# A four-layer graph attention stack: ScalarE issues the 2048-piece reads, GpSimd takes the roots, and the planner counts transfers differently

## The chip, the cores and the metric

The kernel runs on one core of a Trainium2 chip. The metric is the device time of one launch in microseconds (us). Engines are named as in the profile: PE is TensorE (PEld its weight loads), DVE VectorE, ACT ScalarE, POOL GpSimd, SP SyncE, which here only issues DMAs. Each engine executes its own instructions in order and waits on semaphores for the others.

## The reference

128 independent graphs of 128 nodes with 512 features pass through four attention layers. Each layer is an attention over a masked 128x128 score matrix (with 1, 4, 8 and 1 heads), a residual and a layer norm:

```python
x = _layernorm(x + _L0_gnn_ref(x, adj, ...), axis=-1)   # 1 head, no projection, mask adj + I
x = _layernorm(x + _L1_gnn_ref(adj, x, ...), axis=-1)   # 4 heads of 256, elu, then 1 head of 512
x = _layernorm(x + _L2_gnn_ref(x, adj, ...), axis=-1)   # 8 heads of 64
x = _layernorm(x + _L3_gnn_ref(x, adj, ...), axis=-1)   # 1 head of 32 for the scores, elu
```

A layer norm is (x - mean) / sqrt(var + 1e-5) over the 512 features. An attention is, head by head,

```python
e = leaky_relu(s_i[:, None] + s_j[None, :], 0.2)
a = softmax(where(mask, e, -big))
y = a @ h
```

All data are fp32.

## The kernel before

One graph is one tile of 128 partitions (its nodes) by 512 columns. Everything that happens to one graph, from the load of x to the store of the result, is written once in `graph(g)` as a list of `Op`s with an engine, a cost in us, a function that emits the instructions, and the buffers read and written. Some weights are loaded and prepared in a `setup` list, which is interleaved with the first graphs.

The order in which each engine gets its instructions isn't the order of the text. `Pipeline` makes it in two steps, both in Python while the kernel is built:

- `plan` takes one graph and lays its operations on a cycle of `PERIOD` us, by a list schedule with a random shift for each operation (`SEED`, `SPREAD`) and a weight for what is still behind it (`URGENCY`). Graph g gets the same times plus g periods. `Op.done` adds the `LATENCY` of the engine before a reader may start.
- `order` takes the operations of all 128 graphs and the setup and issues them one after the other as an imagined machine would: each engine has a clock, `FLOW` is the latency from one engine to another, `lane` is the one resource that all transfers share (`dma` us each), and a buffer is given to an operation only when a slot is free. An operation may be taken up to `AHEAD` us ahead of the earliest one not yet issued. The sequence that comes out is the instruction stream; on the chip semaphores hold the dependencies, whatever the times turn out to be.

So the constants change no computation, but they change the order on all five engines at once. Some fifteen graphs are under way at any time.

What matters for the change, with line numbers of the profile:

- Attention. `spread` turns a score column into a row through DRAM: a VectorE transpose (L589), a DMA to `row` (L592), a DMA that broadcasts the row to all partitions (L596). `attend` adds the other score and applies the leaky relu on ScalarE (L646, one instruction a head), masks and takes the minimum on VectorE (L654), exponentiates on ScalarE (L663), takes reciprocals (L671) and, for layers 1 and 3, scales on GpSimd (L673).
- Transposes. `turned` transposes 128x128 blocks for TensorE: VectorE transposes 32x32 blocks (L607), SyncE writes them to a DRAM scratch tile `scr` (L612) and reads them back with the blocks in their new places (L622, or L617 where `moving`). With n = 4 the read at L622 is made of 128 x 16 pieces of 32 elements, 2048 in all; there are four of these a graph: the transposed x before the projections at L710 with w1s and with wha, and the two halves of the 8 heads for L938. With n = 1 it has 512 pieces.
- Layer norm. `norm` has statistics on VectorE (L681, L682), the root as exp(-0.5 ln(var + eps)) on ScalarE (L685, L686), -mean times root on GpSimd (L692), and the scaling of the 128x512 tile on ScalarE (L699). There are four a graph.
- Matmuls. L710 projections, L725 mixing with 512 columns, L794 the second matrix of layer 1 (seven products for two graphs in place of eight), L850 the transpose of a mask, L896 and L938 mixing of heads. ScalarE evicts the projections (L717).
- The masks are made on GpSimd from adj (L838, L738), and GpSimd does several 128x512 additions (L780, L862, L881, L950, L986).

Before, SyncE issues every transfer of a graph, 30 in all. A transfer signals one of eight DMA semaphores, taken in turn, so an issue also waits until the transfer eight before it has landed.

Of the kernel before, what the change touches and what calls it, by code (L numbers as in the profile page):

```python
# [29 lines left out]

PERIOD = 28.0
LATENCY = {"PE": (0.0, 0.8), "DVE": (0.15, 1.44), "ACT": (0.1, 1.44), "POOL": (0.1, 1.44), "SP": (7.06, 7.06)}
FLOW = {"PE": (0.0, 0.6), "DVE": (0.15, 0.8), "ACT": (0.1, 0.8), "POOL": (0.1, 0.8), "SP": (4.5, 4.5)}
AHEAD = 20.0
URGENCY = 0.6
BANKS = 8

SEED, SPREAD = 989, 8.0

# [21 lines left out]
class Op:  # L61
# [8 lines left out]
    def done(self, reader=None):  # L70
        own, other = LATENCY[self.engine]
        return self.cost + self.extra + (own if reader is self.engine else other)


class Pipeline:
# [69 lines left out]
    def order(self, events):  # L145

        ops, n = [e[3] for e in events], len(events)
# [33 lines left out]
        known = {e: [i for i in range(n) if not before[i] and ops[i].engine == e] for e in FLOW}  # L181
        issued, low, out = [False] * n, 0, []

        def start(i):
            t = max(clock[ops[i].engine], ready[i])
            for b in makes[i]:

                rank = 0
                for q in coming[b.tag]:
                    if q >= i or rank >= len(free[b.tag]):  # L190
                        break
                    rank += 1
                if rank >= len(free[b.tag]):
                    return None
                t = max(t, free[b.tag][rank][0])
            return t

        while len(out) < n:
            best = None
            for e, waiting in known.items():  # L200
                found = None
                for i in waiting:
                    if events[i][0] > events[low][0] + AHEAD and i != low:
                        break
                    t = start(i)
# [6 lines left out]
            t, i = best  # L212
            op = ops[i]
# [7 lines left out]
            own, other = FLOW[op.engine]  # L221
            if op.engine == "POOL":
                other += op.extra
            if op.dma:

                done = lane = max(lane, done) + op.dma
                own = other = FLOW["SP"][0]
            for q in after[i]:
                ready[q] = max(ready[q], done + (own if ops[q].engine == op.engine else other))
                before[q] -= 1  # L230
                if not before[q]:
                    insort(known[ops[q].engine], q)
# [11 lines left out]
def tile_gat_stack(  # L244
# [50 lines left out]
    nc.scalar.preload_act_table_set("natural_log_exp_and_others")  # L295
    minus = const.tile([P, P], F32, name="minus")
# [270 lines left out]
    def graph(g):  # L567
# [3 lines left out]
        def op(engine, cost, emit, ins=(), outs=(), extra=0.0, uses=(), dma=0.0):  # L571
            ops.append(Op(engine, cost, emit, list(ins), list(outs), extra, uses, dma))
# [7 lines left out]
        def spread(col, nh):  # L580


            sT, row = Buf(f"sT{nh}", [P, nh, 32]), Buf(f"row{nh}", [nh, P])

            def turn():
                c, out = col(), sT.ap
                if len(c.shape) > 2:
                    out = out.rearrange("p (a b) c -> p a b c", a=c.shape[1])
                nc.vector.transpose(out, c.unsqueeze(len(c.shape)).to_broadcast([*c.shape, 32]))  # L589

            op("DVE", 0.12 + 0.033 * nh, turn, [col.buf], [sT])
            op("SP", 0.6, lambda: nc.sync.dma_start(  # L592
                out=row.ap.rearrange("h (b c) -> b h c", b=P // 32), in_=sT.ap[0:P:32]
            ), [sT], [row], dma=0.02 + 0.03 * nh)
            db = Buf(f"db{nh}", [P, nh, P])
            op("SP", 0.4, lambda: nc.sync.dma_start(  # L596
                out=db.ap.rearrange("p h j -> p (h j)"),
                in_=row.ap.rearrange("h j -> (h j)").partition_broadcast(P),
            ), [row], [db], 1.0 + 0.1 * nh, dma=0.03 + 0.19 * nh)
            return db  # L600

        def turned(src, n, moving=False):
# [8 lines left out]
            ), [src], [zb])  # L611
            op("SP", 0.4, lambda: nc.sync.dma_start(  # L612
                out=scr.ap, in_=zb.ap.rearrange("p b h c -> p (b h c)")
            ), [zb], [scr], 0.2 * n, dma=0.05 + 0.17 * n)
# [7 lines left out]
            op("SP", 0.65, lambda: nc.sync.dma_start(  # L622
                out=out.ap.rearrange("p h (q c) -> p h q c", q=4),
# [13 lines left out]
        def attend(db, h0, nh, src, mask, scaled=False):  # L637
# [192 lines left out]
        def first(g):  # L830


            x0, at = Buf("x0", [P, F]), Buf("adj", [P, P], I32)
            op("SP", 0.4, lambda: nc.sync.dma_start(out=x0.ap, in_=x[g]), [], [x0], 1.0, dma=0.72)
            op("SP", 0.4, lambda: nc.sync.dma_start(out=at.ap, in_=adj[g]), [], [at], 1.0, dma=0.22)
            ae = Buf("ae", [P, P], I32)
# [18 lines left out]

            resid(x1, pa, ri, x0)
            norm(x1)


# [4 lines left out]
        def second(g, st, xl):  # L864
# [46 lines left out]
        def third(g, st, xl2):  # L911
# [48 lines left out]

            op("DVE", 0.2, scores, [z3, xl3], [sc4])
            mv, rd = norm(x3, plus=1.0)
# [11 lines left out]
            at, m3 = Buf("adj", [P, P], I32), Buf("m3", [P, P])  # L974
            op("SP", 0.4, lambda: nc.sync.dma_start(out=at.ap, in_=adj[g]), [z3], [at], 1.0, dma=0.22)
            mask(m3, at, ALU.is_equal)
# [10 lines left out]
            norm(y)  # L987
            op("SP", 0.4, lambda: nc.sync.dma_start(out=out[g], in_=y.ap), [y], [], 1.0, dma=0.72)
        if g == B:
# [61 lines left out]
```

## Time and profile before

| | |
|---|---|
| median of 3 runs | 3223.14 us (3217.84 to 3232.31) |
| profiled execution | 3260.22 us, span 3258.4 us |
| mean granted TensorE clock | 0.976 |
| DMA: moved, mean busy share of the queue over 16 engines | 606.08 MB, 75.0% |
| SyncE: transfers issued in its program order | 3873 |
| VectorE waits in all, the longest kind: L744 for x from DRAM | 85.0 us in 71 times |

| us from the start | PE | DVE | ACT | POOL |
|---|---|---|---|---|
| 0 to 100 | 73.47 | 52.14 | 30.91 | 53.83 |
| 100 to 200 | 86.58 | 72.72 | 47.67 | 64.23 |
| 1000 to 1100 | 96.46 | 89.02 | 79.77 | 58.12 |
| 2000 to 2100 | 96.39 | 88.81 | 76.36 | 60.93 |
| 3100 to 3200 | 77.63 | 76.98 | 75.68 | 34.36 |

The second table is busy time in us in stretches of 100 us. The kernel fills for some 200 us, runs evenly to 3100 us, and drains. Every duration below comes from the profiled execution, which took 1.0115 times the median of the runs. Numbers in a group's line are the busy time as a union, the mean of one instruction in ns, and the idle time of the engine just before such instructions. Matmul records come in two for each fp32 matmul.

### The profile page before, as it was taken

The page shows a single profiled execution, that of the slowest core. Times are in us where ns is not written, and L with a number is a line of the kernel's source. Part 1 is how long each engine was busy: PE and PEld are TensorE (multiplying, and loading weights), DVE is VectorE, ACT ScalarE, POOL GpSimd, SP SyncE. Part 2 cuts the span into 40 slices and gives each one's busy share as a digit, 9 for nine tenths or more (in the row PEclk, how much of TensorE's full clock was granted, in tenths as well). Part 3 has the DMA queues.
Part 4 walks back from the last instruction along what each step waited for, and adds up shares of the span by engine and source line. Part 5 has one row for each costly group of instructions (what it writes and reads, how often), then busy time and mean ns, then how long its engine had stood idle before and what let it go on. Part 6 is the DMA issues. An engine that isn't in the chain of part 4 may idle for free. (4 is left out here: it accounts for less than half of the span.)

```text
span 3258.4 us, 62058 instructions
## 1 busy us (share of the span) xinstructions
PE 3066.8 (94%) x14822; PEld 2488.7 (76%) x14822; DVE 2779.0 (85%) x9833; ACT 2451.2 (75%) x8741; POOL 1895.1 (58%) x2347
## 2 busy tenths in 40 slices
PE   6899999999999999999999999999999999999984
PEld 4688887787777877877777778777787777878853
DVE  4779888888888988898888889889898898989875
ACT  2457787787777777787777877777877777778875
POOL 4655655665565655665555665565566556565533
PEclk7899999999999999999999999999999999999985
DMA  4358777877877877877778777877787787777875
GB/s 119 94 136 196 183 205 188 200 193 190 203 187 188 205 186 192 201 190 200 188 187 200 191 188 204 189 190 201 191 204 187 188 205 188 196 196 190 197 174 129
DMA packets 1657567, 606.08 MB, mean 186 GB/s; under 512 B 1311562, under 2 KB 1508170, under 8 KB 1657204
## 3 DMA queue, kind: packets, MB, share of 16 engines
q1 hardware_dynamic: 1655836, 598.97, 75.0%
q8 instruction: 120, 1.97, 0.2%
q14 instruction: 243, 1.99, 0.2%
q0 software_dynamic: 576, 2.10, 0.2%
q10 hardware_dynamic: 792, 1.06, 0.1%
HBM read 374.43 MB, written 227.48 MB: 185 GB/s over the span
## 5 line engine op out<-in xcount | busy, mean ns | idle before, releaser
L710 PE MATMUL ps<-w1s,w 128*128 128x258 f32 x4096 | 926.9, 384 | 48.5 <-DMA w<-scr 25.0
L710 PEld LDWEIGHTS ps<-w1s,w 128*128 128x128 f32 x4096 | 777.0, 191 | 186.3 <-DVE xl L812 39.5
L654 DVE CUSTOM_DVE_ANT_0 w<-w,w 128x128 f32<-128x128 f32 x1920 | 861.1, 544 | 65.6 <-ACT w L646 49.2
L794 PE MATMUL ps<-w2s,w 128*128 128x257 f32 x3584 | 849.0, 383 | 8.5 <-POOL w L780 8.4
L663 ACT ACTIVATE w<-w,nm 128x128 f32<-128x128 f32 x1920 | 748.0, 394 | 98.2 <-DVE nm L654 76.3
L794 PEld LDWEIGHTS ps<-w2s,w 128*128 128x128 f32 x3584 | 669.1, 191 | 188.8 <-issue 80.0
L646 ACT ACTIVATE w<-w,xl 128x128 f32<-128x128 f32 x1536 | 488.8, 389 | 279.9 <-DMA w<-row 259.1
L607 DVE STREAM_TRANSPOSE w<-w 128x512 f32<-128x512 f32 (+1 forms) x1024 | 551.5, 540 | 34.3 <-ACT w L663 13.3
L710 PE MATMUL ps<-wha,w 128*128 128x273 f32 x2048 | 502.3, 398 | 7.3 <-DMA w<-scr 6.9
L710 PEld LDWEIGHTS ps<-wha,w 128*128 128x128 f32 x2048 | 383.2, 192 | 87.4 <-DVE w L607 6.3
L699 ACT ACTIVATE w<-w,mr,rd 128x512 f32<-128x512 f32 x512 | 415.2, 811 | 33.9 <-POOL mr L692 33.0
L692 POOL TENSOR_SCALAR mr<-mv,rd 128x1 f32<-128x1 f32 x512 | 160.1, 313 | 409.4 <-ACT rd L686 201.8
L663 ACT ACTIVATION_READ_ACCUMULATOR w<-w,nm 128x1 f32 x1920 | 368.1, 192 | 0.0
L681 DVE BATCH_NORM_STATS2 st<-w 128x6 f32<-128x512 f32 x512 | 337.2, 668 | 5.4 <-POOL w L986 4.6
L881 POOL TENSOR_TENSOR xl<-xl,b1t 128x512 f32<-128x512 f32 x256 | 335.2, 1310 | 1.6
L938 PEld LDWEIGHTS ps<-xl,w 128*128 128x128 f32 x2048 | 274.3, 196 | 80.8 <-issue 24.4
L646 ACT ACTIVATE w<-w,sc 128x128 f32<-128x128 f32 x384 | 152.3, 397 | 227.6 <-DMA w<-row 226.6
L725 PE MATMUL ps<-w,w 128*128 128x512 f32 x512 | 277.4, 624 | 32.6 <-DMA w<-scr 31.6
L738 POOL TENSOR_SCALAR w<-adj 128x128 f32<-128x128 int32 x256 | 192.4, 752 | 188.2 <-DMA adj<-in_adj_dram 75.1
L717 ACT COPY xl<-ps 128x258 f32<-128x258 f32 (+1 forms) x768 | 273.2, 362 | 31.8 <-PE ps L710 31.3
L938 PE MATMUL ps<-xl,w 128*128 128x66 f32 x2048 | 265.2, 273 | 27.7 <-DMA w<-scr 14.4
L654 DVE DVE_READ_ACCUMULATOR2_ANT nm<- 128x1 f32 x1920 | 290.5, 151 | 0.0
(213 smaller groups left out, 4258.8 us busy)
## 6 DMA issues: line engine op xcount, KB each, us to landing
scr<-w SPq DMA_DIRECT2D x640, 256.0 KB
w<-scr SPq DMA_DIRECT2D x640, 256.0 KB
w<-row SPq DMA_DIRECT2D x128, 512.0 KB
w<-in_x_dram SPq DMA_DIRECT2D x128, 256.0 KB
w<-row SPq DMA_DIRECT2D x128, 256.0 KB
out_dram<-w SPq DMA_DIRECT2D x128, 256.0 KB
w<-row SPq DMA_DIRECT2D x384, 64.0 KB
scr<-w SPq DMA_DIRECT2D x384, 64.0 KB
```

Of the source, the lines that this page charges most:

```text
L607: op("DVE", 0.12 + 0.133 * n, lambda: nc.vector.transpose(zb.ap.rearrange("p b h c -> p h b c"), src.ap.rearrange("p (h b c) -> p h b c", ...
L646: nc.scalar.activation(z.ap[:, h, :], db.ap[:, h0 + h, :], AF.Prelu, bias=src(h0 + h), alpha=SLOPE)
L654: nc.vector.tensor_tensor_reduce(out=zz.ap[:, h, :].rearrange("p (b a) -> p a b", b=4), in0=z.ap[:, h, :].rearrange("p (a b) -> p a b", b= ...
L663: nc.scalar.activation(zz.ap[:, h, :], zz.ap[:, h, :], AF.Exp, bias=nm.ap[:, h : h + 1], scale=-1.0, accum_out=rs.ap[:, h : h + 1],)
L681: op("DVE", 0.6, lambda: nc.vector.bn_stats(st.ap, y.ap), [y], [st])
L699: op("ACT", 0.7, lambda: nc.scalar.activation(y.ap, y.ap, AF.Identity, bias=mr.ap, scale=rd.ap), [y, rd, mr], [y])
L710: op("PE", w * 4 / 2400 + 0.006, lambda k=k: nc.tensor.matmul(px.ap[:, :w], lhsT=lhs.ap[:, k, :], rhs=wa(k, c), start=(k == 0), stop=(k == ...
L717: op("ACT", 0.06 + w / 1200, lambda: nc.scalar.copy(dst(), px.ap[:, :w]), [px], [t])
L725: op("PE", width * 4 / 2400, lambda: nc.tensor.matmul(pa.ap[:, :width] if len(xv.shape) == 2 else pa.ap.rearrange("p (s c) -> p s c", s=2) ...
L794: return lambda: nc.tensor.matmul(q[b].ap[:, :C2], lhsT=x()[:, k, :], rhs=w2s[:, slot, k, :], start=(fresh and k == 0), stop=(k == 3), ski ...
L881: op("POOL", 1.3, lambda nh=nh: nc.gpsimd.tensor_add(xl.ap[:, nh, : 2 * FH], xl.ap[:, nh, : 2 * FH], b1t[:, nh * 2 * FH : (nh + 1) * 2 * F ...
L938: op("PE", 0.225, lambda u=u, h=h: nc.tensor.matmul(pa.ap[:, u * CH : (u + 1) * CH], lhsT=pt.ap[:, u, :], rhs=xl3.ap[:, h * CH : (h + 1) * ...
```

## The change

The reads of `turned` with n = 4 are issued from ScalarE's DMA queue. The root of the layer norm is one addition and one power on GpSimd, and the table preload on ScalarE goes. The first norm of a graph is scaled by one VectorE instruction in place of GpSimd's and ScalarE's. Of the two evictions of the wha projection one goes to VectorE. The planner gets other constants: a period, latencies, urgency and seed; longer costs for issuing transfers; a window of eight transfers (`WINDOW`, `LANDING`) outside which no issue may start; the latency of a transfer for any operation with `dma`, whoever issues it; and new costs for a few operations on GpSimd and VectorE.

```diff
-PERIOD = 28.0
-LATENCY = {"PE": (0.0, 0.8), "DVE": (0.15, 1.44), "ACT": (0.1, 1.44), "POOL": (0.1, 1.44), "SP": (7.06, 7.06)}
-FLOW = {"PE": (0.0, 0.6), "DVE": (0.15, 0.8), "ACT": (0.1, 0.8), "POOL": (0.1, 0.8), "SP": (4.5, 4.5)}
+PERIOD = 30.0
+LATENCY = {"PE": (0.0, 0.8), "DVE": (0.15, 1.76), "ACT": (0.1, 1.76), "POOL": (0.1, 1.76), "SP": (6.98, 6.98)}
+FLOW = {"PE": (0.0, 0.6), "DVE": (0.15, 0.8), "ACT": (0.1, 0.8), "POOL": (0.1, 0.8), "SP": (3.2, 3.2)}
 AHEAD = 20.0
-URGENCY = 0.6
+WINDOW, LANDING = 8, 2.0
+URGENCY = 0.3
 BANKS = 8
-SEED, SPREAD = 989, 8.0
+SEED, SPREAD = 139, 8.0
...
-        own, other = LATENCY[self.engine]
+        own, other = LATENCY["SP" if self.dma else self.engine]
...
             t = max(clock[ops[i].engine], ready[i])
+            if ops[i].dma and ops[i].engine != "POOL" and len(landed) >= WINDOW:
+                t = max(t, landed[-WINDOW])
...
-            if op.engine == "POOL":
-                other += op.extra
             if op.dma:
 
                 done = lane = max(lane, done) + op.dma
                 own = other = FLOW["SP"][0]
+                if op.engine != "POOL":
+                    landed.append(done + LANDING)
+            elif op.engine == "POOL":
+                other += op.extra
...
-    eps = const.tile([P, 1], F32, name="eps")
-    nc.vector.memset(eps, EPS)
-    nc.scalar.preload_act_table_set("natural_log_exp_and_others")
+    neghalf = const.tile([P, 1], F32, name="neghalf")
+    nc.vector.memset(neghalf, -0.5)
...
-            op("SP", 0.6, lambda: nc.sync.dma_start(
+            op("SP", 0.64, lambda: nc.sync.dma_start(
...
-            op("SP", 0.4, lambda: nc.sync.dma_start(
+            op("SP", 0.52, lambda: nc.sync.dma_start(
...
-                op("SP", 0.6, lambda: nc.sync.dma_start(
+                op("SP", 0.52, lambda: nc.sync.dma_start(
...
-            op("SP", 0.65, lambda: nc.sync.dma_start(
+            by, cost, queue = ("ACT", 0.7, nc.scalar) if n == 4 else ("SP", 0.75, nc.sync)
+            op(by, cost, lambda: queue.dma_start(
                 out=out.ap.rearrange("p h (q c) -> p h q c", q=4),
                 in_=flat().rearrange("(q p h c) -> p h q c", q=4, p=P, h=n),
             ), [scr], [out], 1.5, dma=0.415 * n)
...
-                op("POOL", 0.15 + 0.29 * nh, lambda: nc.gpsimd.tensor_mul(
+                op("POOL", 0.15 + 0.22 * nh, lambda: nc.gpsimd.tensor_mul(
...
-        def norm(y, plus=0.0):
+        def norm(y, plus=0.0, on_act=True):
...
             def root():
-                nc.scalar.activation(rd.ap, mv.ap[:, 1:2], AF.Ln, bias=eps)
-                nc.scalar.activation(rd.ap, rd.ap, AF.Exp, scale=-0.5)
-
-            op("ACT", 0.44, root, [mv], [rd])
+                nc.gpsimd.tensor_scalar_add(rd.ap, mv.ap[:, 1:2], EPS)
+                nc.gpsimd.tensor_tensor(out=rd.ap, in0=rd.ap, in1=neghalf, op=ALU.pow)
+
+            op("POOL", 0.95, root, [mv], [rd])
+            if not on_act:
+                op("DVE", 0.45, lambda: nc.vector.tensor_scalar(
+                    out=y.ap, in0=y.ap, scalar1=mv.ap[:, 0:1], scalar2=rd.ap,
+                    op0=ALU.subtract, op1=ALU.mult,
+                ), [y, mv, rd], [y])
+                return
...
-            norm(x1)
+            norm(x1, on_act=False)
...
-                op("POOL", 1.3, lambda nh=nh: nc.gpsimd.tensor_add(
+                op("POOL", 1.36, lambda nh=nh: nc.gpsimd.tensor_add(
...
-            project(xT, lambda k, c: wha[:, k, c * C3 // 2 : (c + 1) * C3 // 2], KF, C3 // 2, xl3, ["ACT", "ACT"],
+            project(xT, lambda k, c: wha[:, k, c * C3 // 2 : (c + 1) * C3 // 2], KF, C3 // 2, xl3, ["DVE", "ACT"],
...
-            op("DVE", 0.2, scores, [z3, xl3], [sc4])
+            op("DVE", 0.7, scores, [z3, xl3], [sc4])
```

The other transfers on SyncE (x, adj, the writes to `scr`, the store) go from a cost of 0.4 to 0.52 in the same way. In the new program order SyncE issues 3361 transfers and ScalarE 512 of those 2048-piece reads.

More of the change, by code (lines that the diff above doesn't have):

```diff
@@ L181, in order @@
         known = {e: [i for i in range(n) if not before[i] and ops[i].engine == e] for e in FLOW}
-        issued, low, out = [False] * n, 0, []
+        issued, low, out, landed = [False] * n, 0, [], []
         def start(i):
             t = max(clock[ops[i].engine], ready[i])
+            if ops[i].dma and ops[i].engine != "POOL" and len(landed) >= WINDOW:
+                t = max(t, landed[-WINDOW])
             for b in makes[i]:
@@ L611, in turned @@
             ), [src], [zb])
-            op("SP", 0.4, lambda: nc.sync.dma_start(
+            op("SP", 0.52, lambda: nc.sync.dma_start(
                 out=scr.ap, in_=zb.ap.rearrange("p b h c -> p (b h c)")
@@ L616, in turned @@
             if moving:
-                op("SP", 0.6, lambda: nc.sync.dma_start(
+                op("SP", 0.52, lambda: nc.sync.dma_start(
                     out=out.ap.rearrange("p h i -> p (h i)").rearrange("p (q e) -> p q e", q=4),
@@ L833, in first @@
             x0, at = Buf("x0", [P, F]), Buf("adj", [P, P], I32)
-            op("SP", 0.4, lambda: nc.sync.dma_start(out=x0.ap, in_=x[g]), [], [x0], 1.0, dma=0.72)
-            op("SP", 0.4, lambda: nc.sync.dma_start(out=at.ap, in_=adj[g]), [], [at], 1.0, dma=0.22)
+            op("SP", 0.52, lambda: nc.sync.dma_start(out=x0.ap, in_=x[g]), [], [x0], 1.0, dma=0.72)
+            op("SP", 0.52, lambda: nc.sync.dma_start(out=at.ap, in_=adj[g]), [], [at], 1.0, dma=0.22)
             ae = Buf("ae", [P, P], I32)
@@ L974, in third @@
             at, m3 = Buf("adj", [P, P], I32), Buf("m3", [P, P])
-            op("SP", 0.4, lambda: nc.sync.dma_start(out=at.ap, in_=adj[g]), [z3], [at], 1.0, dma=0.22)
+            op("SP", 0.52, lambda: nc.sync.dma_start(out=at.ap, in_=adj[g]), [z3], [at], 1.0, dma=0.22)
             mask(m3, at, ALU.is_equal)
@@ L987, in third @@
             norm(y)
-            op("SP", 0.4, lambda: nc.sync.dma_start(out=out[g], in_=y.ap), [y], [], 1.0, dma=0.72)
+            op("SP", 0.52, lambda: nc.sync.dma_start(out=out[g], in_=y.ap), [y], [], 1.0, dma=0.72)
         if g == B:
```

## The prediction

> **What bounds the kernel now.** I read the busy shares first, then a long steady stretch cut out of the span, then what TensorE waits for in it, then how the other engines lose time.
>
> ```profile
> PE 3066.8 (94%) x14822; PEld 2488.7 (76%) x14822; DVE 2779.0 (85%) x9833; ACT 2451.2 (75%) x8741; POOL 1895.1 (58%) x2347
> ```
>
> ```profile
> 300.00:3000.00 2700.00, 2609.49 (x12856) 2135.26 (x12855) 2376.62 (x8493) 2115.03 (x7597) 1613.76 (x2008) 1.00 0.79 194
> ```
>
> The columns of the second line are PE, PEld, DVE, ACT and POOL busy us, then clock, DMA share and GB/s. One graph has 115 matmul records (32+28+16+16+16+6+1 from the groups' counts divided by 128), so 12856 records are 111.8 graphs: 24.15 us a graph, in which PE is busy 23.34, DVE 21.26, ACT 18.92, POOL 14.43. PE idles 90.5 us of the 2700, 0.81 us a graph. TensorE bounds the kernel, and nothing can save more than 0.81 x 128 = 104 us outside fill and drain.
>
> ```profile
> PE ps L710 <- DMA w<-scr: 25.0, 24, 2.1
> PE ps L725 <- DMA w<-scr: 15.2, 27, 1.3
> PE ps L850 <- DVE w L903: 15.0, 15, 1.9
> PE ps L710 <- DVE ri L671: 9.3, 9, 2.1
> PE ps L710 <- DVE st L681: 8.4, 5, 2.0
> ```
>
> These are TensorE's waits from 300 to 3000 us (total, times, longest). 40.2 us hang on reads of transposed data, of which 25.0 on the 2048-piece ones (L710); most of the rest hangs on VectorE. At 85 to 88% busy, VectorE is next after TensorE, and part of its busy time is no work:
>
> ```profile
> L654 DVE CUSTOM_DVE_ANT_0 w<-w,w x1920: 328/382/1522, 33.4 to 3241.2; 128x128 f32<-128x128 f32 x192
> L959 DVE TENSOR_TENSOR sc<-sc,xl x128: 160/563/1201, 264.6 to 3231.0; 128x2 f32<-128x2 f32 x128
> ```
>
> ```profile
> 1002.07 1.27 POOL L780 TENSOR_TENSOR w<-w,w 128x512 f32<-128x512 f32 x1
> 1002.09 0.15 DVE L654 DVE_READ_ACCUMULATOR2_ANT nm<- 128x1 f32 x1
> 1002.09 1.50 DVE L654 CUSTOM_DVE_ANT_0 w<-w,w 128x128 f32<-128x128 f32 x1
> ```
>
> Min/median/max in ns: the same 128x128 masking takes 0.33 us or 1.5 us, and the long one began just as GpSimd's 1.27 us tensor_tensor did. Its mean is 544 ns in the groups, so 1920 x (544-382) = 311 us are excess; L959 adds 128 x (638-160) = 61 us, two elements wide as it is.
>
> Last, the issuing:
>
> ```profile
> 1005.02 0.64 SPq L622 DMA_DIRECT2D w<-scr  x1
> ```
>
> ```profile
> 0.73 1.28 ACT L295 ACT_TABLE_LOAD   x1 [0.73 <-PEq L1037]
> 0.77 0.53 ACTq L318 DMA_DIRECT2D w_-1_1_95<-in_L_gnn_attn_w_dst_dram  x1
> ```
>
> ```profile
> ACT w L646 <- DMA w<-row: 485.7, 319, 7.8
> ```
>
> A 2048-piece read holds SyncE 0.64 us, plus about 0.1 us between two issues (gaps of 0.03 to 0.05 us around a short semaphore instruction). ScalarE's sequencer can issue a DMA while its engine works (0.77 lies inside the table load). And ScalarE already waits 485.7 us, in order, for broadcast rows.
>
> **What the Trainium skill says.** "SBUF — State Buffer", section "SBUF: two separate sides": VectorE and GpSimd share a port pair under an exclusive lock; a VectorE instruction with two SBUF inputs, or in a two-port mode, and a GpSimd one shut each other out for the whole instruction. The trace agrees (0.33 against 1.50 us). "DMA: Bandwidth & Descriptors", section "Issuing engines are not separate DMA queues": a second issuing engine saves only the sequencer's issue time. The trace has nearly all transfers on one queue, so it can't say; I take it that data flows no faster. "VectorE: DVE Perf Modes", section "Mode 2×_2P": fp32 tensor_scalar from SBUF can do two elements a cycle; no steady instruction here shows it.
>
> **The change, part by part.** Sums stand against the profiled execution, 3260.22 us (span 3258.4), 1.0115 times the median of 3223.14; I divide by that at the end.
>
> *Reads to ScalarE.* 512 issues (4 a graph) leave SyncE: 512 x 0.74 = 379 us of its queue, 12% of the span. ScalarE gets them: between 0, where the issue lies under a running activation, and 379 us; I take 0.64 x 512 = 328, because each also waits for its write to land and for one of the eight semaphores, with evictions and exps queued behind it.
>
> *Roots to GpSimd.* ScalarE loses 146.4 + 103.8 = 250 us (L685, L686). GpSimd gets 512 adds at 0.27 us (L692's median for one column) and 512 powers. No power runs in the trace: at least 0.27 us like the add, at most 0.68, which would make the pair the 0.95 us booked for it in the code. I take 0.5: 512 x 0.77 = 394 us (276 to 486). One hop between engines goes (VectorE, GpSimd, ScalarE in place of VectorE, ScalarE, GpSimd, ScalarE); the chain's work is 0.49 us before and 0.77 after, so its length hardly moves.
>
> *First norm on VectorE, one L710 eviction of wha to VectorE.* ScalarE loses 128 x 0.811 + 128 x 0.369 = 151 us, GpSimd 128 x 0.313 = 40. VectorE gets 128 tensor_scalars of 128x512: 0.33 us at two a cycle (estimate, 512/0.96 GHz/2 + 60 ns, from the page's clock and rate) to 0.73 (L733, the nearest row); I take 0.45, so 58 us. And 128 copies of 273 columns at 0.40 (L812 moves 257 in 0.404): 51 us.
>
> *The lock.* GpSimd goes from 1895 to 1895+394-40 = 2249 us, 19% more. The excess of 311+61 = 372 us on VectorE grows between 0 (short instructions block briefly) and 19%, 71 us; I take 50.
>
> *Sums per engine.* ScalarE 2451-250-151+328 = 2378. GpSimd 2249 (69%). SyncE gains 379. VectorE 2779+58+51+50 = 2938, +1.24 us a graph: 22.50 of 24.15, 93%. TensorE's work is the same, matmul for matmul.
>
> *The order.* All queues are reordered, so single waits can't be followed across. What the two instruction orders tell: a tile's running number counts tiles placed so far, some 350 a graph, so the distance from a read's tile to its first matmul is a share of a graph. For the 512-wide mixing (L725) the nearest distances go from 0.21 to 0.45 of a graph, for the mask transpose (L850) from 0.27 to 0.35; for the w1 projection (L710, the largest wait) from 0.285 to 0.286. For ScalarE's four-head L646, which waits for broadcasts, the median falls from 0.265 to 0.18, or 6.4 to 4.4 us. So TensorE gets more room at two of its three waits, and ScalarE less. The lag from a graph's mask transpose to its last mixing stays (15.86 to 15.62 graphs of TensorE work), so fill and drain stay: nothing booked.
>
> *Queue for queue.* The most that earlier reads give is 40.2 x 128/111.8 = 46 us. Against it stands VectorE's room: 24.15-21.26 = 2.89 us idle a graph now, 1.24 of it taken. If VectorE's waits shrink by all 1.24, nothing is lost; if by none, 1.24 x 128 = 159 us. Much of its idle time is being early, for x (85.0 us at L744) or a free row tile (51.7 at L589), and that shrinks; waits inside chains with ScalarE and TensorE don't. I choose that five sixths are absorbed: 0.20 us a graph lost, 26 us, with the reads' gain used up by VectorE coming later to evictions and residuals. So 3260+26 = 3286, over 1.0115: **3249 us**.
>
> **Rivals.** *A, the reads win:* VectorE's idle time takes all 1.24 us and TensorE loses its read waits: 3260-46 = 3214, 3177 us by the median (3150 to 3207). For it: TensorE's stalls are short (2.1 us at most) and the order gives them room; chains behind them are mostly transfers. Against: it needs TensorE at 98% and VectorE at 94 to 95% in one in-order machine with eight PSUM banks. *B, a wash:* a read can't start before its write has landed, whoever issues it, and the wait moves along: 3223. For it: SyncE's L622 waited for its write only 26.7 us in all, so SyncE was seldom the cause. *C, ScalarE becomes late:* L646 sits behind 2 us less distance and a blocking read. If half of its 768 waits for broadcasts cost 0.5 us more and TensorE pays half of that, +96 us: 3318. It decides once ScalarE's 24.15-18.6 = 5.6 us of room, of which 3.8 are those waits now, is full. Against: ScalarE's sum falls by 73 us.
>
> **How the numbers follow.** Forecast 0.37 (3240 to 3300), A 0.35, B 0.18, C 0.10. The forecast and C are slower, A faster. What this measurement can tell from no change is about 0.5%, 16 us: so 0.35 faster, 0.18 the same, 0.47 slower. Both signs hold much of it, so the range goes from within A (3165, with some 0.1 below) to the start of C (3315).
>
> **What would show it.** VectorE's share in the steady stretch at 92 to 94%, L654's mean above 544 ns, GpSimd near 69%: the load is right. TensorE's waits for w<-scr under 20 us with waits for VectorE at 60 or more: the forecast. Both small, steady period under 23.9 us: A. ScalarE's wait for w<-row over 800 us and its evictions ending TensorE's waits: C. A power of well over 0.68 us, or fill and drain off by more than 15 us, would make the sums wrong.

## The result, and the profile after

The changed kernel takes 3272.20 us (median of 4 runs, 3270.86 to 3275.53) against 3224.68 us for the kernel before in runs on the same chip: a ratio of 1.0148, 95% interval [1.0124, 1.0173]. That is 48 us slower, beyond the 0.5% that the measurement can tell. The profiled execution of the changed kernel, 3275.53 us, is close to its median; that of the kernel before was 1.1% above its own, so the two traces differ by 15 us only, and the ratio of the runs is what counts.

The busy shares on the page of the changed kernel:

```profile
PE 3058.9 (93%) x14822; PEld 2487.3 (76%) x14822; DVE 3054.1 (93%) x10089; ACT 2171.7 (66%) x7461; POOL 2279.4 (70%) x3243
```

Its steady stretch (PE, PEld, DVE, ACT, POOL busy us, clock, DMA share, GB/s):

```profile
300.00:3000.00 2700.00, 2583.69 (x12780) 2120.34 (x12779) 2632.03 (x8654) 1868.30 (x6440) 1936.25 (x2771) 1.00 0.79 193
```

12780 records are 111.1 graphs, 24.30 us each. VectorE is busy 97.5% of the stretch, 23.68 us a graph; TensorE 95.7%. VectorE, not TensorE, is now the engine that sets the pace, and TensorE's waits in the same stretch (total us, times, longest) say the same:

```profile
PE ps L806 <- DVE xl L727: 94.1, 54, 3.9
PE ps L806 <- POOL w L792: 19.3, 47, 0.7
PE ps L908 <- ACT xl L729: 2.2, 5, 0.9
```

No wait for a read (w<-scr) is left. TensorE waits instead for one eviction on VectorE, the one that the change moved there. VectorE's groups by shape (count, busy us, mean ns, idle before) tell how it filled up:

```profile
L660 DVE CUSTOM_DVE_ANT_0 w<-w,w 128x128 f32<-128x128 f32 x1920 | 930.5, 577 | 10.5 <-ACT w L652 10.2 <-issue 0.2
...
L971 DVE TENSOR_TENSOR sc<-sc,xl 128x2 f32<-128x2 f32 x128 | 104.0, 813 | 4.4
...
L696 DVE TENSOR_SCALAR w<-w,mv,rd 128x512 f32<-128x512 f32 x128 | 71.2, 556 | 5.5 <-POOL rd L692 5.0
...
L727 DVE COPY xl<-ps 128x273 f32<-128x273 f32 x128 | 51.8, 404 | 17.1 <-PE ps L722 17.1
```

VectorE's busy time rose by 3054.1 - 2779.0 = 275 us. The two new rows, L696 and L727, are 71.2 + 51.8 = 123 us of it. The other 152 us are instructions that were there before and take longer. Four groups make nearly all of it: the maskings (L654 before, L660 now), a custom instruction with three inputs and 512 columns (L744, now L756) and two additions of two elements (L915 and L959, now L927 and L971). Before:

```profile
L654 DVE CUSTOM_DVE_ANT_0 w<-w,w 128x128 f32<-128x128 f32 x1920 | 861.1, 544 | 65.6 <-ACT w L646 49.2 <-DMA row<-w 11.2 <-ACT w L663 3.8
L744 DVE CUSTOM_DVE_ANT_0 w<-w,w0s,b0t 128x512 f32<-128x512 f32 x128 | 102.2, 798 | 0.2 <-issue 0.2
L959 DVE TENSOR_TENSOR sc<-sc,xl 128x2 f32<-128x2 f32 x128 | 81.6, 638 | 4.4
L915 DVE TENSOR_TENSOR sc<-xl,shift 128x2 f32<-128x2 f32 x128 | 27.6, 215 | 0.0
```

and now, beside the lines for L660 and L971 above:

```profile
L756 DVE CUSTOM_DVE_ANT_0 w<-w,w0s,b0t 128x512 f32<-128x512 f32 x128 | 149.1, 1165 | 0.0
L927 DVE TENSOR_TENSOR sc<-xl,shift 128x2 f32<-128x2 f32 x128 | 82.0, 641 | 0.0
```

These four rose by 69, 47, 22 and 54 us; that is more than 152 together, since instructions overlap in time and a few others became shorter.

### The profile page after: what moved, and what is told of

Its sections match the earlier page's. It is cut to its first block, busy times and chain, and to the rows that moved or that the text cites. A ratio compares the mean times of both kernels' runs of the same rounds, so it can differ in the third digit from the quotient of the medians.

```text
span 3273.7 us, 62684 instructions
## 1 busy us (share of the span) xinstructions
PE 3058.9 (93%) x14822; PEld 2487.3 (76%) x14822; DVE 3054.1 (93%) x10089; ACT 2171.7 (66%) x7461; POOL 2279.4 (70%) x3243
## 5 line engine op out<-in xcount | busy, mean ns | idle before, releaser
L806 PE MATMUL ps<-w2s,w 128*128 128x257 f32 x3584 | 865.7, 385 | 118.1 <-DVE xl L727 94.1
L722 PE MATMUL ps<-w1s,w 128*128 128x258 f32 x4096 | 949.8, 383 | 7.3 <-DMA w<-scr 7.3
L660 DVE CUSTOM_DVE_ANT_0 w<-w,w 128x128 f32<-128x128 f32 x1920 | 930.5, 577 | 10.5 <-ACT w L652 10.2
L806 PEld LDWEIGHTS ps<-w2s,w 128*128 128x128 f32 x3584 | 659.0, 190 | 258.3 <-DVE xl L727 116.1
L711 ACT ACTIVATE w<-w,mr,rd 128x512 f32<-128x512 f32 x384 | 313.9, 819 | 78.7 <-POOL mr L708 59.5
L962 POOL TENSOR_TENSOR w<-z,w 128x512 f32<-128x512 f32 x128 | 151.4, 1183 | 273.0 <-DVE z L954 238.8
L893 POOL TENSOR_TENSOR xl<-xl,b1t 128x512 f32<-128x512 f32 x256 | 326.8, 1286 | 4.7
L692 POOL TENSOR_TENSOR rd<-rd,neghalf 128x1 f32<-128x1 f32 x512 | 298.0, 582 | 42.6
L691 POOL TENSOR_SCALAR rd<-mv 128x1 f32<-128x1 f32 x512 | 137.3, 268 | 246.0 <-DVE mv L688 167.0
L908 PEld LDWEIGHTS ps<-w,xl 128*128 128x128 f32 x2048 | 249.6, 192 | 63.3 <-issue 46.4
L660 DVE DVE_READ_ACCUMULATOR2_ANT nm<- 128x1 f32 x1920 | 286.9, 149 | 0.0
```

Of the source, the lines that this page charges most:

```text
L660: nc.vector.tensor_tensor_reduce(out=zz.ap[:, h, :].rearrange("p (b a) -> p a b", b=4), in0=z.ap[:, h, :].rearrange("p (a b) -> p a b", b= ...
L692: nc.gpsimd.tensor_tensor(out=rd.ap, in0=rd.ap, in1=neghalf, op=ALU.pow)
L711: op("ACT", 0.7, lambda: nc.scalar.activation(y.ap, y.ap, AF.Identity, bias=mr.ap, scale=rd.ap), [y, rd, mr], [y])
L722: op("PE", w * 4 / 2400 + 0.006, lambda k=k: nc.tensor.matmul(px.ap[:, :w], lhsT=lhs.ap[:, k, :], rhs=wa(k, c), start=(k == 0), stop=(k == ...
L806: return lambda: nc.tensor.matmul(q[b].ap[:, :C2], lhsT=x()[:, k, :], rhs=w2s[:, slot, k, :], start=(fresh and k == 0), stop=(k == 3), ski ...
L893: op("POOL", 1.36, lambda nh=nh: nc.gpsimd.tensor_add(xl.ap[:, nh, : 2 * FH], xl.ap[:, nh, : 2 * FH], b1t[:, nh * 2 * FH : (nh + 1) * 2 * ...
```

## The experiments

Two questions came out of this: what the single parts of the change are worth, and why VectorE's old instructions became longer. The first four kernels undo parts of the change with the changed kernel's order kept: the planner still counts the engine and cost of the change, and only the emitted instruction differs. The next two make one part alone in the order of the kernel before, and two more lighten VectorE in either order. The last four look for what makes VectorE slow. Ratios are to the kernel before, with their 95% intervals.

### The parts undone, in the new order

**Roots back on ScalarE.**

```diff
-                nc.gpsimd.tensor_scalar_add(rd.ap, mv.ap[:, 1:2], EPS)
-                nc.gpsimd.tensor_tensor(out=rd.ap, in0=rd.ap, in1=neghalf, op=ALU.pow)
+                nc.scalar.activation(rd.ap, mv.ap[:, 1:2], AF.Ln, bias=eps)
+                nc.scalar.activation(rd.ap, rd.ap, AF.Exp, scale=-0.5)
```

> The changed kernel with its program order kept, and the roots emitted on ScalarE again (two activations in place of GpSimd's addition and power). Theory V (VectorE became the bound, and a good part of its new busy time is waiting for the port pair that GpSimd holds): GpSimd loses 435 us, VectorE's busy time falls by 100 to 200 us from 3054 although none of its instructions changes, and the time falls to 3150 to 3210. Theory V without the lock (only the moved instructions made VectorE slow): VectorE's busy time stays within 30 us and the time within 3255 to 3275. Theory O (the new order itself makes the waits, whatever the engines carry): 3260 to 3285.

Measured: 3247.29 us, 1.0071 [1.0044, 1.0098]. GpSimd falls from 2279 to 1876 us busy, VectorE only from 3054 to 3021. The time lies between the bands of the three theories, in none of them. Without the roots on GpSimd VectorE is 33 us less busy and the kernel some 25 us faster; half of the loss stays. The 33 us are a net figure: the additions at L927 became 48 us shorter and the maskings 40 us longer, so taking the roots away also changed when the other instructions meet.

**First scaling and the wha eviction back on ScalarE.**

```diff
-                op("DVE", 0.45, lambda: nc.vector.tensor_scalar(
-                    out=y.ap, in0=y.ap, scalar1=mv.ap[:, 0:1], scalar2=rd.ap,
-                    op0=ALU.subtract, op1=ALU.mult,
+                op("DVE", 0.45, lambda: nc.scalar.activation(
+                    y.ap, y.ap, AF.Identity, bias=rd.ap[:, 1:2], scale=rd.ap[:, 0:1]
...
-                    op("DVE", 0.05 + w / 960, lambda: nc.vector.tensor_copy(dst(), px.ap[:, :w]), [px], [t])
+                    op("DVE", 0.05 + w / 960, lambda: nc.scalar.copy(dst(), px.ap[:, :w]), [px], [t])
```

> The changed kernel with its program order kept, the first norm's scaling and the eviction of the first half of wha emitted on ScalarE again; roots stay on GpSimd, which also gets the 128 products of mean and root. Theory V: 123 us leave VectorE, which was busy 97.5% of the steady stretch, so the time falls by 80 to 125 us, to 3147 to 3192. Theory L (the lock is all that matters): GpSimd carries 34 us more, so 3265 to 3285. Theory O: 3260 to 3285.

Measured: 3273.44 us, 1.0151 [1.0114, 1.0188]: no gain, though VectorE's busy time fell by 124 us. Of this kernel the waits of all engines in the steady stretch:

```profile
DVE w L611 <- ACT w L701: 151.7, 111, 3.5
...
PE ps L912 <- ACT xl L733: 78.4, 59, 2.4
...
PE ps L810 <- ACT xl L731: 4.8, 10, 1.1
```

The order had been made for a scaling that sits on VectorE just ahead of the transpose that reads it. With the scaling on ScalarE the transpose waits 1.4 us for it, 111 times. TensorE hardly waits for the moved eviction any more (L731), but 78.4 us for the evictions that ScalarE had all along (L733), which the new work in its queue seems to delay. This run doesn't measure the moved work; it swaps it for waits.

**All three back.** Both edits together, so that every engine executes what it did before, in the new order and with the reads on ScalarE.

> Both edits together: all compute is on the engines of the kernel before, only the program order and ScalarE's issuing of reads are those of the changed kernel. Theory V: VectorE is back at 2750 to 2800 us busy, TensorE bounds the kernel again and its waits for w<-scr are small, so 3150 to 3195, faster than before. Theory O: no faster than before, 3225 or more.

Measured: 3349.51 us, 1.0388 [1.0354, 1.0422]. Theory V, which had VectorE back at 2750 to 2800 us and the kernel faster than before, has fallen. The same new waits explain part of the time. But the page of this kernel has a line that the others make important:

```profile
PE 3100.0 (92%) x14822; PEld 2491.8 (74%) x14822; DVE 3001.9 (89%) x9833; ACT 2487.8 (74%) x8741; POOL 1902.1 (57%) x2347
```

VectorE executes the same 9833 instructions as before, and GpSimd the same 2347, and VectorE needs 3002 us for what took 2779. Neither engine got any work. The reads on ScalarE don't explain it either: alone, in the order of before, they leave VectorE at 2760 us (below). The excess is made by the order.

**Reads back on SyncE.**

```diff
-            by, cost, queue = ("ACT", 0.7, nc.scalar) if n == 4 else ("SP", 0.75, nc.sync)
+            by, cost, queue = ("ACT", 0.7, nc.sync) if n == 4 else ("SP", 0.75, nc.sync)
```

> The changed kernel with its program order kept, the 2048-piece reads issued by SyncE. Theory V: reads aren't what is waited for, so the time stays within 3262 to 3285. Theory R (ScalarE's issuing is a gain that VectorE's load only hides): TensorE's waits for w<-scr come back and the time goes over 3290. Theory C (reads that block ScalarE's queue cost time): below 3255.

Measured: 3280.36 us, 1.0166 [1.0135, 1.0198], no difference from the changed kernel that its interval can tell. TensorE's longest wait is the changed kernel's:

```profile
PE ps L806 <- DVE xl L727: 96.0, 54, 4.1
```

In this order, where VectorE sets the pace, it doesn't matter who issues the reads.

### One part alone, in the order of before

**Roots on GpSimd alone.** The first diff, turned round, in the kernel before.

> The kernel before, its program order kept, with the roots emitted on GpSimd. Theory V: VectorE's excess grows by some 0.4 us a graph, as it fell by 0.37 when the changed kernel lost its roots, inside its 2.9 us of room: 3225 to 3255. Theory L (the roots' hold on the port pair is what costs): VectorE's busy time grows by 150 us or more and the time goes over 3265.

Measured: 3226.63 us, 1.0004 [0.9993, 1.0016]. GpSimd goes up by 416 us and VectorE by 17 (2779.0 to 2796.0): nothing.

**Reads on ScalarE alone.**

```diff
-            op("SP", 0.65, lambda: nc.sync.dma_start(
+            queue = nc.scalar if n == 4 else nc.sync
+            op("SP", 0.65, lambda: queue.dma_start(
```

> The kernel before, its program order kept, with the 2048-piece reads issued by ScalarE. Theory R (earlier reads are worth TensorE's waits for them): 3180 to 3212. Theory V: SyncE's issuing was seldom the cause, 3212 to 3240. Theory C (a blocked ScalarE queue costs): over 3245, with more time in which ScalarE's evictions end TensorE's waits.

Measured: 3144.02 us, 0.9753 [0.9737, 0.9770]. This is the fastest version of the study that leaves nothing out, 79 us under the kernel before, and below every band that was expected. Its steady stretch:

```profile
300.00:3000.00 2700.00, 2692.45 (x13445) 2239.51 (x13444) 2462.19 (x8865) 2235.89 (x7948) 1671.24 (x2087) 1.00 0.83 202
```

TensorE is busy 99.7%: 116.9 graphs pass where 111.8 did. PE's own busy time for a graph fell too, from 23.34 to 23.03 us. These are all its waits in that stretch, in the same columns as above:

```profile
PE ps L726 <- ACT xl L718: 2.5, 9, 0.3
PE ps L711 <- ACT xl L718: 2.0, 5, 0.8
PE ps L726 <- DMA w<-scr: 1.7, 1, 1.7
PE ps L795 <- POOL w L781: 0.6, 1, 0.6
PE ps L939 <- DMA w<-scr: 0.5, 1, 0.5
```

Not only the waits for reads are gone, those for VectorE are as well, without one VectorE instruction changed. What SyncE had been doing is not on the page, which doesn't count issuing as busy. The timeline of the kernel before has it (start us, duration us); the first line follows directly on the read at 1005.02 that the prediction shows:

```profile
1005.76 2.00 SPq L592 DMA_DIRECT2D row<-sT  x1
1007.86 0.39 SPq L596 DMA_DIRECT2D w<-row  x1
...
1039.18 3.08 SPq L592 DMA_DIRECT2D row<-sT  x1
```

The issue after a 2048-piece read takes 2.00 and 3.08 us in place of half a microsecond. The durations of L592 (min/median/max ns), before:

```profile
L592 SPq DMA_DIRECT2D row<-sT x512: 482/538/4098, 17.8 to 3234.5; - x171
```

and with the reads on ScalarE:

```profile
L592 SPq DMA_DIRECT2D row<-sT x512: 476/514/1669, 17.8 to 3118.5; - x171
```

Counted over the whole trace of before: of the 512 issues that directly follow a 2048-piece read, 503 take over 0.8 us; of the 256 that follow a 512-piece read at the same line, 3; of the 3104 others, 101. SyncE's issue durations add up to 2659 us of the 3258 before and to 1511 with the four reads moved, while ScalarE's rise by 338. From the start of such a read's issue to the end of a stretched one behind it there are 2.4 us in the median, where 0.64 us and half a microsecond would have been 1.2.

One thing else changed with the issuing engine: the moved reads run on a DMA queue of their own (packets, MB, share of 16 engines). Before:

```profile
q1 hardware_dynamic: 1655836, 598.97, 75.0%
q10 hardware_dynamic: 792, 1.06, 0.1%
```

and with the reads on ScalarE:

```profile
q1 hardware_dynamic: 599068, 464.72, 50.8%
q10 hardware_dynamic: 1057560, 135.31, 27.7%
```

So the other transfers no longer stand behind the pieces of the reads in one queue. No run separates this from the time that SyncE gained; either would make transfers come earlier.

**VectorE's load, in both orders.** The statistics of all four norms over 128 of the 512 columns, in the changed kernel and, as a control, in the kernel before.

```diff
-            op("DVE", 0.6, lambda: nc.vector.bn_stats(st.ap, y.ap), [y], [st])
+            op("DVE", 0.6, lambda: nc.vector.bn_stats(st.ap, y.ap[:, :P]), [y], [st])
```

> The changed kernel, same order, same engines, same waits; the statistics of all four norms are taken over the first 128 of the 512 columns, which leaves out three quarters of four VectorE instructions a graph (0.67 us to about 0.27 us each, 1.6 us a graph) and adds no wait. The two earlier edits that took work off VectorE gave it to ScalarE in a place made for VectorE, and VectorE then waited for ScalarE. Theory V (VectorE, 97.5% busy, sets the pace): 24.3 us a graph falls until TensorE's 23.3 to 23.5 bind, so 3150 to 3200. Theory O (a handover fixed by the order, such as the PSUM bank between the wha eviction and L806, sets the pace): within 15 us of 3272.

> The same shortening of the statistics in the kernel before: the control. Theory V: there TensorE sets the pace and VectorE has 2.9 us of room a graph, so the time falls by 0 to 30 us, 3195 to 3228. Theory W (VectorE's load counts in any order, since it delays what TensorE waits for): it falls by as much as in the changed kernel, 70 us or more.

Measured: in the changed kernel 3210.39 us, 0.9962 [0.9943, 0.9982], 62 us less, with VectorE's busy time down by 110 us; in the kernel before 3217.58 us, 0.9982 [0.9970, 0.9995], 6 us less, with VectorE down by 182 us. The first lies 10 us above the band of theory V and far from that of O: some 205 us of work left VectorE, but its old instructions took 95 back, the maskings with 608 ns in place of 577. The second lies within the band of V. VectorE's busy time is worth time after the change and almost none before it.

### What makes VectorE slow

**The order of before, with every move of the change.** Roots on GpSimd and reads on ScalarE as above, one wha eviction and the first scaling on VectorE; TensorE and SyncE have the order of before, instruction for instruction, SyncE without the reads. The scaling stands where ScalarE's stood in the order, and GpSimd still makes -mean times root for it.

```diff
-            op("ACT", 0.7, lambda: nc.scalar.activation(
+            op("ACT", 0.7, (lambda: nc.scalar.activation(
                 y.ap, y.ap, AF.Identity, bias=mr.ap, scale=rd.ap
-            ), [y, rd, mr], [y])
+            )) if on_act else (lambda: nc.vector.tensor_scalar(
+                out=y.ap, in0=y.ap, scalar1=rd.ap, scalar2=mr.ap, op0=ALU.mult, op1=ALU.add
+            )), [y, rd, mr], [y])
...
-                    op("ACT", 0.06 + w / 1200, lambda: nc.scalar.copy(dst(), px.ap[:, :w]), [px], [t])
+                    copy = nc.vector.tensor_copy if w == C3 // 2 and c == 1 else nc.scalar.copy
+                    op("ACT", 0.06 + w / 1200, lambda: copy(dst(), px.ap[:, :w]), [px], [t])
```

> The order of before, instruction for instruction on TensorE and SyncE, with every move of the change in place: roots on GpSimd, first scaling and one eviction of the wha projection on VectorE, 2048-piece reads issued by ScalarE. VectorE then executes what it executes in the changed kernel (some 2.85 to 2.9 ms before waits on the ports). Theory 'order' (the new order, not the work it moves, makes VectorE slow): VectorE's busy time stays at 2880 to 2940 us, 0.98 to 1.00 of before, 3155 to 3225 us. Theory 'load' (the moved work alone makes VectorE the limit): VectorE's busy time at 3000 us or above, 3250 us or more. The run with the reads alone on ScalarE took 3144 us.

Measured: 3181.76 us, 0.9858 [0.9835, 0.9882], inside the band of the order theory; VectorE's 2950.4 us lie 10 above that band and 50 below that of the load theory. The page of this kernel:

```profile
PE 3038.0 (96%) x14822; PEld 2495.7 (79%) x14822; DVE 2950.4 (93%) x10089; ACT 2151.8 (68%) x7461; POOL 2317.8 (73%) x3371
```

and VectorE's moved scaling and its maskings by shape:

```profile
L653 DVE CUSTOM_DVE_ANT_0 w<-w,w 128x128 f32<-128x128 f32 x1920 | 855.0, 543 | 17.6 <-ACT w L645 17.3
...
L700 DVE TENSOR_SCALAR w<-w,rd,mr 128x512 f32<-128x512 f32 x128 | 97.2, 759 | 11.8 <-POOL mr L691 11.8
```

Nearly the same moves that cost 48 us in the new order leave a gain of 46 in the old one, and the maskings stay at 543 ns. With the reads alone at 0.9753 this splits the change, taken in this sequence: reads -0.0247, moves +0.0105, order +0.0290 of 3225 us, that is -80, +34 and +94, in all +48. Another sequence would split it otherwise, since the reads are worth nothing measurable once the order is the new one.

**Another seed.** The changed kernel, with its operations, engines and costs as they are, and one constant of the planner different.

```diff
-SEED, SPREAD = 139, 8.0
+SEED, SPREAD = 14, 8.0
```

> The changed kernel with another seed of the planner (14 for 139): the same operations on the same engines with the same costs, in another order. Theory 'this order' (the loss is an accident of one order): VectorE's busy time differs by 60 us or more and the time by more than 1%. Theory 'load and balance' (any order with this balance has VectorE as its pace): VectorE's busy time 3000 to 3100 us, time 3240 to 3320 us.

Measured: 3167.74 us, 0.9820 [0.9795, 0.9845]; VectorE 2872.7 us, 181 less. The theory that any order with this balance must lose has fallen: one other draw gains 1.8%.

**GpSimd's two largest additions cut.** No VectorE instruction differs from the changed kernel.

```diff
-                    xl.ap[:, nh, : 2 * FH], xl.ap[:, nh, : 2 * FH], b1t[:, nh * 2 * FH : (nh + 1) * 2 * FH]
+                    xl.ap[:, nh, :32], xl.ap[:, nh, :32], b1t[:, nh * 2 * FH : nh * 2 * FH + 32]
...
-            op("POOL", 1.3, lambda: nc.gpsimd.tensor_add(y.ap, y.ap, x3.ap), [y, x3], [y])
+            op("POOL", 1.3, lambda: nc.gpsimd.tensor_add(y.ap[:, :32], y.ap[:, :32], x3.ap[:, :32]), [y, x3], [y])
```

> The changed kernel with GpSimd's bias addition to the second layer's projection and its last residual addition cut to 32 columns; the rest of these two additions is left out. No VectorE instruction differs. Theory 'port' (VectorE's instructions grow because GpSimd holds the port pair that both use): VectorE's busy time falls by 60 us or more, the 128x128 sums of L660 come down from 577 towards 544 ns, time 3190 to 3240 us. Theory 'load' (VectorE is slow by its own count of work): VectorE's busy time within 20 us of 3054, time above 3255 us.

Measured: 3119.92 us, 0.9670 [0.9644, 0.9696], below what even the port theory gave. Its maskings:

```profile
L660 DVE CUSTOM_DVE_ANT_0 w<-w,w 128x128 f32<-128x128 f32 x1920 | 654.0, 434 | 12.3 <-ACT w L652 11.3 <-POOL w_-1_39_492 L476 0.7 <-issue 0.2
```

577 to 434 ns, and VectorE's busy time from 3054.1 to 2728.7 us: GpSimd's additions had made VectorE's instructions long. What was left to ask is whether it is the ports or simply that GpSimd was done earlier, and which addition. The timeline of the changed kernel answered the second:

```profile
1517.25 1.32 POOL L792 TENSOR_TENSOR w<-w,w 128x512 f32<-128x512 f32 x1
1517.39 1.42 DVE L660 CUSTOM_DVE_ANT_0 w<-w,w 128x128 f32<-128x128 f32 x1
...
1518.53 1.31 POOL L998 TENSOR_TENSOR w<-w,w 128x512 f32<-128x512 f32 x1
...
1518.67 1.41 DVE L660 CUSTOM_DVE_ANT_0 w<-w,w 128x128 f32<-128x128 f32 x1
...
1519.93 0.37 DVE L660 CUSTOM_DVE_ANT_0 w<-w,w 128x128 f32<-128x128 f32 x1
```

Two maskings, each begun 0.14 us after a GpSimd addition, end 0.24 us after it; the third, with no addition beside it, takes 0.37 us. The first addition, L792, lay on maskings before too. The second, L998, the last residual, is new there. Counted over each trace, how many of its 128 instances lie over a masking by more than 0.9 us: before 2, the order of before with all moves 2, the changed kernel 114 (and 113 to 115 in the five kernels that keep its order and its additions), the other seed 26. It isn't the only meeting that changed. The bias addition at L881, now L893, went from 60 of 256 to 126; the scaling at L673, now L679, from 84 of 128 to 1, and the residual at L862, now L874, from 47 of 128 to 1. These two now stand on other instructions: 107 of the 128 at L756 began while L679 was running, and the 54 at L927 that began under L874 took 1.24 us, against 0.16 us for the 55 that began under a root's one-column addition.

All 1920 maskings of a trace can be sorted by what GpSimd does beside them (number, mean ns, how many over 0.9 us):

| | before | changed |
|---|---|---|
| nothing | 897, 376, 0 | 386, 376, 0 |
| one-column instructions alone | 165, 376, 0 | 568, 364, 0 |
| a wider one that began before the masking | 636, 881, 310 | 763, 890, 395 |
| a wider one that began after it | 222, 380, 1 | 203, 379, 0 |

With one exception a masking is long only where it found a wide GpSimd instruction under way, and in the changed kernel 127 more of them did.

**The last addition's time kept, little data moved.**

```diff
-            op("POOL", 1.3, lambda: nc.gpsimd.tensor_add(y.ap, y.ap, x3.ap), [y, x3], [y])
+            def added():
+                nc.gpsimd.tensor_add(y.ap[:, :16], y.ap[:, :16], x3.ap[:, :16])
+                nc.gpsimd.tensor_tensor(out=spare, in0=two, in1=neghalf, op=ALU.pow)
+                nc.gpsimd.tensor_scalar_add(spare, two, EPS)
+                nc.gpsimd.tensor_add(y.ap[:, 16:32], y.ap[:, 16:32], x3.ap[:, 16:32])
+
+            op("POOL", 1.3, added, [y, x3], [y])
```

> The changed kernel with GpSimd's last residual addition (L998, 128x512, 1.29 us, 128 times) replaced by work of the same length on GpSimd that moves little data: two additions of 16 columns (about 0.25 us each) around one power and one addition of 128x1 (0.58 and 0.22 us). The residual of the other 480 columns is left out. GpSimd's busy time stays within 30 us of 2279. Theory 'one collision' (in the new order this addition lies on VectorE's 128x128 sums and holds the port that they need): VectorE's busy time falls by 80 to 150 us, L660 from 577 to 500 to 525 ns, time 3150 to 3220 us. Theory 'GpSimd late' (what counts is when GpSimd gets done, not what it holds): nothing changes, 3255 to 3290 us.

Measured: 3156.84 us, 0.9804 [0.9777, 0.9830], 115 us under the changed kernel. The page:

```profile
PE 3035.7 (96%) x14822; PEld 2491.4 (79%) x14822; DVE 2916.4 (92%) x10090; ACT 2156.3 (68%) x7461; POOL 2269.2 (72%) x3627
```

GpSimd is as busy as it was (2269 against 2279 us); VectorE is 138 us less busy, 123 of them in the maskings:

```profile
L662 DVE CUSTOM_DVE_ANT_0 w<-w,w 128x128 f32<-128x128 f32 x1920 | 807.5, 513 | 11.1 <-ACT w L654 9.9 <-POOL w_-1_39_495 L478 0.7 <-issue 0.4
```

and TensorE's wait for the eviction is down from 94.1 us:

```profile
PE ps L808 <- DVE xl L729: 22.3, 50, 2.4
```

So it is what GpSimd holds, not when it is done. One addition, once a graph, at the wrong place in the order cost 115 us, more than the 94 by which the whole order was dearer; the order's other meetings, better and worse ones, weren't taken apart.

## Why the prediction came out, and where it was wrong

*The time and the mechanism.* 3249 us were forecast, 3272 came, within the range; "slower" had the highest chance. The signs that the forecast named are there: waits for w<-scr under 20 us (none), for VectorE at 60 or more (94.1), the maskings above 544 ns (577), GpSimd near 69% (70%). VectorE's share is 97.5% in the steady stretch where 92 to 94% had been named. That VectorE's load would eat up what earlier reads give was right. That the time came within 23 us was luck: the reads' gain and the cost of the order were both far larger than booked, one of each sign.

*The reads' gain, mis-sized: 46 us booked at most, 79 measured alone.* The sum counted the waits that carry the read's name. In the run with the reads alone TensorE's waits for VectorE went as well, and as only the queue was changed, they too had come from late transfers. The prediction's other bound, all of TensorE's idle time (104 us), lies above the 79, but isn't quite a bound: in the traces' steady stretch a graph's period fell by 1.05 us, more than its 0.81 us of idle time, because PE's busy time fell as well. The step that failed with it is "512 x 0.74 = 379 us of its queue": the next issue's stretch belonged to it, and 1149 us of SyncE's issuing disappeared. That this time, and not the reads' own queue, made the transfers earlier is likely but not shown. The stretch could have been seen: the issue right after the quoted line lasts 2.00 us. Rival B's ground, that L622 waited only 26.7 us for its write, looked at the read and not at what stood behind it.

*The lock, mis-sized: 50 us booked (0 to 71), 152 measured.* The bound let the excess grow with GpSimd's busy time. In the old order that nearly holds: with all moves VectorE's sum is 2950.4 - 2760.0 (reads alone) - 97.2 - 52.5 = 41 us above its new work, and some 33 more if the scaling, 759 ns in the mean there, is counted at its shortest, 497. In the new order it doesn't hold, because the excess depends on which instructions meet. The prediction costed the order by the room between reads and matmuls, the loads and the drain. The meeting of VectorE's and GpSimd's instructions wasn't costed at all; the order came to 94 us, and a single meeting in it to 115.

*VectorE's sum: 2938 forecast, 3054 measured.* The excess on old instructions is 102 of the missing 116 us. The first scaling is 556 ns where 450 were taken, and 501 at its shortest, where the estimate at two elements a cycle was 330: 13 us more. The copy is 404 ns as taken.

*Absorption.* Five sixths of 1.24 us a graph absorbed was a choice, and at about this size it wasn't wrong: the moves cost 34 us in the old order, 26 were booked. The load that came was 2.42 us a graph, and the forecast was nearly right because the reads' gain and the order's cost, for which it booked nothing in the end, came near to cancelling.

*The roots.* The power takes 582 ns where 500 were taken, the pair 435 us where 394 were, GpSimd 2279 where 2249 were. In the old order this costs nothing.

*ScalarE.* 2378 forecast, 2172 on the page. The forecast's sum has 328 us of issuing in it, which the page doesn't count; without them it is 2050. Part of the rest is that the roots' 250 us took only 182 off ScalarE's busy time in the run that moved them alone; the remainder wasn't followed up. Rival C didn't come: ScalarE's wait for rows in the steady stretch fell from 443.3 us to 113.9. In the order of before the reads alone took it to 0.8; in the new order it is 149.3 even with the reads back on SyncE, so there most of the fall is the order's. (The 768 in the rival's sum are calls of the attention; the trace has 319 waits.)

*Left open.* Which of the planner's constants put L998 on the maskings wasn't tried, only that a seed takes most of it away. Why an issue behind a 2048-piece read is stretched wasn't tried either, nor how much of the reads' gain is SyncE's time and how much their own queue.

## What to carry to other kernels

Sum up the durations of the issuing instructions of each queue, too: an engine that only issues can be full, and the price of a transfer of many pieces may stand in the instruction behind it. When VectorE and GpSimd both work on SBUF, a new order must be read for which of their instructions lie side by side, since nearly the same work was 94 us dearer in another order, and one addition of it cost 115. And an edit undone in an order made for it measures the waits that it opens, not the work that it saves.

## What the runs showed of the hardware

- The issue of a 2048-piece read lasts 0.59 us on ScalarE and 0.64 on SyncE in the median, but the issue right behind it on SyncE took over 0.8 us in 503 of 512 cases, up to 4 us and more; behind a 512-piece read in 3 of 256. The Trainium skill ("DMA: Bandwidth & Descriptors", section "Issuing engines are not separate DMA queues") says that a second issuing engine saves only the sequencer's time, usually small beside the transfer. Here that time wasn't small for the kernel: SyncE's issuing fell by 1149 us and ScalarE's rose by 338, and 79 us of the kernel's time went. Whether nothing but the sequencer's time counted, no run here shows.
- The page "SBUF — State Buffer", section "SBUF: two separate sides", says that VectorE, with two inputs from SBUF or in a two-port mode, and GpSimd lock a shared pair of ports: whoever starts first has it for its whole instruction. The traces agree. In the changed kernel maskings that began under a wide GpSimd instruction took 890 ns in the mean, those that began before one 379, those alone 376. In the kernel before, too, 310 of the 311 maskings of over 0.9 us had begun under one.
- One-column instructions on GpSimd didn't hold up a masking: the 568 that had only such beside them took 364 ns. Each root adds two of them, an addition and a power of 0.27 and 0.58 us in the mean.
